# A state-space mixer's decay matmuls: two heads in one product, and the block between a sequence's two tiles for all heads at once

## The chip, the cores and the metric

The kernel runs on one core of a Trainium2 chip. It is one launch with everything in float32. The metric is device time in microseconds (us): the median of three runs.

## The reference, cut to what matters

The whole program is two transformer-like blocks, eight layers in a row. The change lies in the third layer, a state-space mixer. It has two passes ahead of it (a recurrent layer and a layer of eight experts) and five behind it. Of this layer the reference computes, for 4 sequences of 256 positions, 8 heads of width 64, and a state of width 64:

```
dt = softplus(dt + dt_bias);  A = -exp(A_log)
D_res = D[:, None] * h                     # skip path, per head
h = h * dt[..., None];  A_d = A * dt       # A_d: one decay exponent per position and head
L = exp(segment_sum(A_d))                  # L[l, s] = exp(sum of A_d over s < k <= l), 0 for s > l
y[l] = sum over s <= l of (C[l] . B[s]) * L[l, s] * h[s]   + D_res[l]
yn = norm_w * rmsnorm(y * silu(gate));  out = yn @ out_proj_w.T
```

The reference does the middle line in chunks of 32 positions and carries states between chunks; written out for a whole sequence it is the sum above. `B` and `C` are the same for all heads; the decay `L` differs by head.

## The kernel before, in words

The 1024 tokens are two groups (`g`), each of two sequences (`b`) of 256 positions; a sequence is two tiles of 128 positions on the 128 partitions. `NH` is 8, `NT` (tiles of a group) is 4. A pass of the mixer's last loop over one group and one sequence is called a **block** here; there are four: (g0,b0), (g0,b1), (g1,b0), (g1,b1).

Ahead of the blocks, each group has its convolution, its gate `sg` and its steps `dt` and exponents `ad` (`dtdt` and `dtad` in the profile). In the last loop a group first transposes `h` and forms `hdt` = h*dt (L365) and `hd` = D*h (L367).

A block then does this:

- `pG` (L373, L375): the products B.C for the three 128x128 pieces of the lower triangle: tile 0 to tile 0, tile 0 to tile 1, tile 1 to tile 1. `Gm` (L378) is that with the causal mask `m384` (called `m` in the profile), 384 columns wide.
- For each of the 8 heads, POOL scales the mask by the head's exponents into `au` (L394, 256 columns; L396, 128 columns). TensorE sums them along the positions into `pS`: L400 with the matrix `strict` (256 columns), L401 with `ones` (128 columns, adds the whole second tile's part to the middle piece), L402 with `strict` (128 columns). ScalarE takes the exponential (L404), VectorE multiplies by `Gm` (L405), and three matmuls of 64 columns (L383, L385, L387, the function `apply`) put the head's result into `pY[0]` and `pY[1]`. `apply` runs two heads behind the making of `L`.
- The tail: `yf` = pY + hd (L415, VectorE), times the gate (L417, POOL), the squares' sum (L419, ScalarE), `rs` (POOL, L101), transposes of `yf` (L430), their copies (L435), the output projection `pob` (L442, recorded under the helper's line L142), and the add to `x` (L443).

A float32 matmul is recorded as two TensorE instructions, so 32 matmuls of L400 appear as x64. `au` and `L` have four buffers each. PSUM tiles come from five banks in rotation (`mm_tile`), the two accumulators `pY` from three others.

The order of instructions on each engine isn't that of the text. A scheduler of the language lays them out when the kernel is built, by readiness under modelled durations. The trace shows it: POOL makes `au` for the next block's first heads ahead of this block's L417, and VectorE's normalisation of the next layer's input (`xn_f`, L117) for group 0 stands between two L405 of block (g1,b0). [...]

What comes after the mixer is a second pass of the eight-expert layer (L0f), whose instructions are laid out by the same scheduler, and then the second half of the program, whose order is written out by hand. The change touches neither.

Of the kernel before, what the change touches and what calls it, by code (L numbers as in the profile page):

```python
# [17 lines left out]
P = 128  # L18
# [4 lines left out]
S = 256  # L23
NT = TG // P
# [6 lines left out]
NH, HP, NS = 8, 64, 64  # L31
# [6 lines left out]
def two_blocks(ctx: ExitStack, tc: tile.TileContext, a: dict, out: bass.AP):  # L38
    nc = tc.nc

    const = ctx.enter_context(tc.tile_pool(name="const", bufs=1))
    small = ctx.enter_context(tc.tile_pool(name="small", bufs=3))
# [4 lines left out]
    def bank(tag, name):  # L47
        return ps.tile([P, 512], F32, tag=tag, name=name, bufs=banks_of[tag])
# [8 lines left out]
    def mm_tile(name, parts=P):  # L57
        return bank("mm" if mm_only[0] else next(mm_turn), name)[:parts]

    def acc_tile(name):  # L60
        return bank(next(acc_turn), name)
# [37 lines left out]
    def rsqrt(dst, src, n):  # L99

        nc.gpsimd.tensor_tensor(dst, src, neghalf[:, :n], ALU.pow)  # L101
# [37 lines left out]
    def project(dst, w, rhs, n=NC):  # L139

        for c in range(n):
            nc.tensor.matmul(dst, w(c), rhs(c), start=(c == 0), stop=(c == n - 1))  # L142
# [148 lines left out]
    def l0_attn_b(pool, win, wout, cw, nw, m384, strict, ones):  # L291
# [38 lines left out]
        for g in range(NG):  # L330
            v = keep[g][1]

            def new(n):
                return small.tile([P, NT, NH], F32, tag=f"dt{n}", name=f"dt{n}_{g}")
# [3 lines left out]
            z, w1, ln, eq, dt, ad = (new(n) for n in ("z", "w1", "ln", "eq", "dt", "ad"))  # L338
# [15 lines left out]
        for g in range(NG):  # L354
            hT, _, sg = keep[g]
            dt, ad = steps[g]
            hdt = pool.tile([P, NT, NH, HP], F32, tag="hdt", name=f"hdt_{g}")
            hd = pool.tile([P, NT, NH, HP], F32, tag="hd", name=f"hd_{g}")
            for t in range(NT):
                ph = mm_tile(f"ph_{g}_{t}")  # L360
                for j in range(4):
                    nc.tensor.transpose(
                        ph[:, j * P:(j + 1) * P], hT[j][:, t * P:(t + 1) * P], ident)
                ph = ph.rearrange("p (h q) -> p h q", h=NH)
                nc.vector.tensor_tensor(  # L365
                    hdt[:, t], ph, dt[:, t, :].unsqueeze(2).to_broadcast([P, NH, HP]), ALU.mult)
                nc.vector.tensor_tensor(  # L367
                    hd[:, t], ph, dres.unsqueeze(2).to_broadcast([P, NH, HP]), ALU.mult)
            for b in range(2):
                s0, s1 = b * S, b * S + P  # L370
                BT, CT = hT[4], hT[5]
                pG = mm_tile(f"pG_{g}_{b}")
                nc.tensor.matmul(pG[:, :S], BT[:, s0:s0 + P], CT[:, s0:s0 + S],  # L373
                                 start=True, stop=True)
                nc.tensor.matmul(pG[:, S:S + P], BT[:, s1:s1 + P], CT[:, s1:s1 + P],  # L375
                                 start=True, stop=True)
                Gm = pool.tile([P, S + P], F32, tag="Gm", name=f"Gm_{g}_{b}")
                nc.vector.tensor_tensor(Gm, pG[:, :S + P], m384, ALU.mult)  # L378
                pY = [acc_tile(f"pY{i}_{g}_{b}") for i in range(2)]

                def apply(h, L):
                    hs = slice(h * HP, (h + 1) * HP)
                    nc.tensor.matmul(pY[0][:, hs], L[:, :P], hdt[:, 2 * b, h, :],  # L383
                                     start=True, stop=True)
                    nc.tensor.matmul(pY[1][:, hs], L[:, P:S], hdt[:, 2 * b, h, :],  # L385
                                     start=True, stop=False)
                    nc.tensor.matmul(pY[1][:, hs], L[:, S:], hdt[:, 2 * b + 1, h, :],  # L387
                                     start=False, stop=True)

                behind = []  # L390
                for h in range(NH):
                    n = f"{g}_{b}_{h}"
                    au = pool.tile([P, S + P], F32, tag="au", name=f"au_{n}", bufs=4)
                    nc.gpsimd.tensor_scalar(  # L394
                        au[:, :S], m384[:, :S], ad[:, 2 * b, h:h + 1], None, ALU.mult)
                    nc.gpsimd.tensor_scalar(  # L396
                        au[:, S:], m384[:, S:], ad[:, 2 * b + 1, h:h + 1], None, ALU.mult)

                    pS = mm_tile(f"pS_{n}")
                    nc.tensor.matmul(pS[:, :S], strict, au[:, :S], start=True, stop=False)  # L400
                    nc.tensor.matmul(pS[:, P:S], ones, au[:, S:], start=False, stop=True)  # L401
                    nc.tensor.matmul(pS[:, S:S + P], strict, au[:, S:], start=True, stop=True)  # L402
                    L = pool.tile([P, S + P], F32, tag="L", name=f"L_{n}", bufs=4)
                    nc.scalar.activation(L, pS[:, :S + P], AF.Exp)  # L404
                    nc.vector.tensor_tensor(L, L, Gm, ALU.mult)  # L405
                    behind.append((h, L))
                    if len(behind) > 2:
                        apply(*behind.pop(0))
                for h, L in behind:
                    apply(h, L)  # L410
                ss = small.tile([P, 2], F32, tag="ss", name=f"ss_{g}_{b}")
                yf = pool.tile([P, 2, DI], F32, tag="yf", name=f"yf_{g}_{b}")
                for i in range(2):
                    t = 2 * b + i
                    nc.vector.tensor_tensor(  # L415
                        yf[:, i, :], pY[i], hd[:, t].rearrange("p h q -> p (h q)"), ALU.add)
                    nc.gpsimd.tensor_tensor(yf[:, i, :], yf[:, i, :], sg[:, t, :], ALU.mult)  # L417
# [499 lines left out]
    with ExitStack() as l0:  # L917
# [37 lines left out]
        with tc.tile_pool(name="b0", bufs=2) as pool:  # L955
            l0_attn_b(pool, win, wout, cw, nw, m384, strict, ones)
# [223 lines left out]
```

## Time and profile before

| what | value |
|---|---|
| median of 3 runs | 1007.36 us (1006.69 to 1009.06) |
| profiled execution, its own time | 1040.18 us |
| span of the profiled execution | 1038.5 us |
| mean granted TensorE clock over the span | 0.912 |
| TensorE busy | 854.4 us (82%) |
| VectorE, ScalarE, POOL busy | 529.0, 256.3, 280.9 us |
| mixer's four blocks, from the first `pS` to the last `pob` | about 194 to 296 us of the span |
| in the stretch 194 to 297 us: TensorE busy, POOL busy, mean clock | 89.84 us, 58.96 us, 0.83 |

How to read it: the profile is one execution, and its own time is 1.7 us more than its span, and 32.8 us more than the median of the runs without a profile. Busy time of TensorE is modelled at its ends, so the starts of successive instructions are the safer measure of what one costs. A line of a timeline gives the start in us, the duration in us, the engine, the source line, the operation, what it writes and reads, the shapes, the count, and in brackets how long the engine was idle before and what released it. "PEclk" in a window is the share of full speed that the clock of TensorE was granted.

### The profile page before, as it was taken

To read this page: it belongs to the slowest core of one execution; us is meant where nothing else is said; L and a number is where in the kernel's file an instruction comes from. 1 tells how busy PE (TensorE), PEld (TensorE's weight loads), DVE (VectorE), ACT (ScalarE), POOL (GpSimd) and SP (SyncE) were. 2 spreads that over 40 slices of the span, in tenths; PEclk is the share of its full clock that TensorE was granted. 3 is DMA by queue.
4 is the path that set the end of the run, shared out by engine and by line. 5 is a ranking of instruction groups with operands and counts; after the bars stand their busy time and mean duration, and the time that the engine had idled before them with its cause. 6 is when DMAs were issued, how large, how long until landed. Compare 5 with 4: busy or idle time off the path is not lost.

```text
span 1038.5 us, 10670 instructions
## 1 busy us (share of the span) xinstructions
PE 854.4 (82%) x3400; PEld 517.6 (50%) x3400; DVE 529.0 (51%) x1570; ACT 256.3 (25%) x470; POOL 280.9 (27%) x344
## 2 busy tenths in 40 slices
PE   4469999988989978988999776978988999866960
PEld 2235444777854433334337655854334336755850
DVE  5876666734346646326434433557525633523532
ACT  3410017522210021222225112212322224311210
POOL 3110000666410040120620325034120441144205
PEclk9779999988789979999999978989999999978995
DMA  8750000000000093000113526621000112435733
GB/s 296 247 183 0 1 0 1 1 1 1 1 1 1 0 265 101 1 21 1 66 46 112 157 98 192 183 86 56 1 0 1 47 66 71 128 126 167 208 109 98
DMA packets 61550, 81.47 MB, mean 78 GB/s; under 512 B 5928, under 2 KB 52528, under 8 KB 60976
## 3 DMA queue, kind: packets, MB, share of 16 engines
q1 hardware_dynamic: 43760, 52.48, 16.4%
q0 software_dynamic: 6144, 16.79, 5.1%
q10 hardware_dynamic: 11584, 11.46, 3.2%
q8 instruction: 29, 0.48, 0.2%
q14 instruction: 33, 0.27, 0.1%
HBM read 42.96 MB, written 37.75 MB: 78 GB/s over the span
## 4 chain that ended last, share of the span: by engine, by line
PE 61%; DVE 14%; issue 10%; POOL 6%; DMA 3%; ACT 3%; another core or an unknown queue 2%; POOLq 0%; ACTq 0%; SPq 0%; DVEq 0%
PE pe_f L142 11%; PE pgu_f L142 6%; PE pST_a L590 4%; PE py_f L841 3%; PE pS_a L555 3%; PE pST_b L590 3%; PE pS_b L555 2%; PE pob L142 2%; PE pcv L142 2%; PE pctx_a L606 2%; DVE ye_f L849 2%; DVE junk_b L561 2%; PE pctx_b L606 2%; PE po_a L142 2%
## 5 line engine op out<-in xcount | busy, mean ns | idle before, releaser
L142 PE MATMUL pgu_f<-gu,xT_f 128*128 128x192 f32 x512 | 107.2, 356 | 12.0 <-DVE ye_f L849 5.5
L142 PE MATMUL pe_f<-L0f_W_sb,xnT_f 128*128 128x512 f32 x256 | 115.7, 600 | 0.0
L142 PEld LDWEIGHTS pgu_f<-gu,xT_f 128*128 128x128 f32 x512 | 88.8, 203 | 23.6 <-DVE ye_f L849 18.1
L866 POOL DMA_INDIRECT yb_f<-done,bk_f x64 | 66.8, 1044 | 113.8 <-DMA xe_f<-sent 47.5
L284 DVE SCALAR_TENSOR_TENSOR x<-pe_f,comb_f,x 128x256 f32<-128x256 f32 x128 | 61.9, 484 | 39.6 <-PE pe_f L142 36.3
L783 POOL DMA_INDIRECT sent<-xn_f,to_f x64 | 63.0, 984 | 69.6 <-DVE full L770 51.5
L142 PEld LDWEIGHTS pe_f<-L0f_W_sb,xnT_f 128*128 128x128 f32 x256 | 46.6, 190 | 53.9 <-issue 51.6
L841 PE MATMUL py_f<-dw,hT_f 96*128 96x256 f32 x256 | 71.9, 408 | 1.5 <-ACT xT_f L818 1.2
L845 DVE TENSOR_TENSOR he_f<-he_f,pgu_f 128x192 f32<-128x192 f32 x64 | 22.5, 352 | 79.2 <-ACT he_f L835 65.0
L561 DVE CUSTOM_DVE_ANT_0 junk_a<-pS_a,tri 128x128 f32<-128x128 f32 (+1 forms) x128 | 45.8, 358 | 27.9 <-PE pS_a L555 22.2
L818 ACT COPY xT_f<-px_f 128x512 f32<-128x512 f32 x64 | 37.3, 586 | 89.2 <-PE px_f L815 67.3
L849 DVE COPY ye_f<-py_f 128x512 f32<-128x512 f32 x64 | 44.2, 691 | 26.7 <-PE py_f L841 9.6
L561 DVE CUSTOM_DVE_ANT_0 junk_b<-pS_b,tri 128x128 f32<-128x128 f32 (+1 forms) x128 | 45.8, 358 | 22.8 <-PE pS_b L555 17.1
L841 PEld LDWEIGHTS py_f<-dw,hT_f 96*128 96x128 f32 x256 | 50.0, 205 | 8.6 <-ACT xT_f L818 1.5
L590 PE MATMUL pST_a<-qm_a,kb_a 128*128 128x512 f32 x96 | 49.8, 625 | 5.3 <-DVE qm_a L577 4.6
L590 PE MATMUL pST_b<-qm_b,kb_b 128*128 128x512 f32 x96 | 49.3, 620 | 5.2 <-DVE qm_b L577 4.6
L595 POOL TENSOR_SCALAR_AFFINE_SELECT pT_a<-pT_a 128x512 f32<-128x512 f32 x32 | 20.4, 640 | 117.0 <-ACT pT_a L593 117.0
L593 ACT ACTIVATE pT_a<-pST_a 128x512 f32<-128x512 f32 x48 | 28.6, 597 | 92.4 <-PE pST_a L590 91.3
L593 ACT ACTIVATE pT_b<-pST_b 128x512 f32<-128x512 f32 x48 | 28.6, 597 | 90.6 <-PE pST_b L590 87.3
L815 PE MATMUL px_f<-ident,xe_f 128*128 128x128 f32 x256 | 41.3, 289 | 11.5 <-DMA xe_f<-sent 10.0
L555 PE MATMUL pS_b<-kb_b,qT_b 128*128 128x512 f32 x96 | 47.7, 601 | 2.8 <-DVE nmx L561 1.8
L555 PE MATMUL pS_a<-kb_a,qT_a 128*128 128x512 f32 x96 | 48.5, 609 | 1.0 <-DVE nmx L561 1.0
(297 smaller groups left out, 1436.4 us busy)
## 6 DMA issues: line engine op xcount, KB each, us to landing
xe_f<-sent SPq DMA_DIRECT2D x64, 256.0 KB
done<-ye_f SPq DMA_DIRECT2D x64, 256.0 KB
sent<-nil ACTq DMA_DIRECT2D x18, 512.0 KB
gu<-in_L1f_gate SPq DMA_DIRECT2D x4, 768.0 KB
gu<-in_L1f_up SPq DMA_DIRECT2D x4, 768.0 KB
dw<-in_L1f_down SPq DMA_DIRECT2D x4, 768.0 KB
L0f_W_sb<-in_L0f_W SPq DMA_DIRECT2D x4, 512.0 KB
L0b_in_sb<-in_L0b_in SPq DMA_DIRECT2D x1, 1160.0 KB
```

The costliest lines, as they stand in the source:

```text
L142: nc.tensor.matmul(dst, w(c), rhs(c), start=(c == 0), stop=(c == n - 1))
L284: nc.vector.scalar_tensor_tensor(x[g][:, t, :], pe[:, h * D:(h + 1) * D], comb[:, t, e:e + 1], x[g][:, t, :], ALU.mult, ALU.add)
L555: nc.tensor.matmul(pS.rearrange("p (s k) -> p s k", s=per), qT[:, c, q0:q0 + P], kb[:, s0:s0 + per, b * S:b * S + w], start=True, stop=True)
L561: nc.vector.tensor_tensor_reduce(out=junk[:, :w], in0=pS[:, i * w:(i + 1) * w], in1=tri[:, S - w:], scale=1.0, scalar=NEG, op0=ALU.add, op ...
L590: nc.tensor.matmul(pS, kb[:, s, k0:k0 + P], qm.rearrange("p c q -> p (c q)"), start=True, stop=True)
L593: nc.scalar.activation(pT.rearrange("p c q -> p (c q)"), pS, AF.Exp)
L606: nc.tensor.matmul(sums[0][32 * s:32 * s + 32, :], v[:, 2 * b + kt, s, :], told.pop(AG * kt + s).rearrange("p c q -> p (c q)"), start=(kt ...
L783: nc.gpsimd.indirect_dma_start(out=sent_to[g][t * TOPK + j], out_offset=bass.IndirectOffsetOnAxis(ap=to[:, t, j:j + 1], axis=0), in_=xn[:, ...
L815: nc.tensor.transpose(px[:, j * P:(j + 1) * P], xe[q][:, k, c * P:(c + 1) * P], ident)
L841: nc.tensor.matmul(py[:, k * D:(k + 1) * D], hT[q][:, k, :], dw[:, 2 * q + k, :], start=True, stop=True)
L849: nc.vector.tensor_copy(ye.rearrange("p k d -> p (k d)"), py)
L866: nc.gpsimd.indirect_dma_start(out=yb, out_offset=None, in_=done[g], in_offset=bass.IndirectOffsetOnAxis(ap=back[:, t, j:j + 1], axis=0), ...
```

## The change

Per group, two small matmuls and one exponential make `reach`: for each tile and head, the decay from a position to the end of its tile, and from the start of a tile to a position. The middle piece (tile 0 to tile 1) is then done for all heads in one matmul `pO` of 512 columns: its left factor is applied to `hdt` ahead of it (`left`, POOL), its right factor after it (`off`, VectorE), and the result is added to `hd`, the skip path. Per pair of heads, one POOL product makes `au` with 512 columns (two heads, two diagonal pieces), one matmul of 512 columns with `strict` makes `pS`, one exponential and one product follow, and `apply` has two matmuls per head instead of three, one pair behind. The matmul with `ones` is gone. `au` and `L` have three buffers of 512 columns instead of four of 384.

```diff
+            pe = mm_tile(f"pe_{g}").rearrange("p (k h) -> p k h", h=NH)
+            nc.tensor.matmul(pe[:, :NT], strict, ad, start=True, stop=True)
+            nc.tensor.matmul(pe[:, NT:2 * NT], m384[:, :P], ad, start=True, stop=True)
+            reach = small.tile([P, 2 * NT, NH], F32, tag="reach", name=f"reach_{g}")
+            nc.scalar.activation(reach, pe[:, :2 * NT], AF.Exp)
...
+                left = pool.tile([P, NH, HP], F32, tag="left", name=f"left_{g}_{b}")
+                nc.gpsimd.tensor_tensor(
+                    left, hdt[:, 2 * b],
+                    reach[:, 2 * b, :].unsqueeze(2).to_broadcast([P, NH, HP]), ALU.mult)
                 pY = [acc_tile(f"pY{i}_{g}_{b}") for i in range(2)]
...
+                def apply(h0, L):
+                    for h in (h0, h0 + 1):
+                        hs = slice(h * HP, (h + 1) * HP)
+                        for i in range(2):
+                            nc.tensor.matmul(pY[i][:, hs], L[:, h - h0, i, :],
+                                             hdt[:, 2 * b + i, h, :], start=True, stop=True)
+
+                behind = []
+                for h in range(0, NH, 2):
+                    n = f"{g}_{b}_{h}"
+                    au = pool.tile([P, 2, 2, P], F32, tag="au", name=f"au_{n}", bufs=3)
+                    nc.gpsimd.tensor_tensor(
+                        au, m384[:, :P].unsqueeze(1).unsqueeze(1).to_broadcast([P, 2, 2, P]),
+                        ad[:, 2 * b:2 * b + 2, h:h + 2].rearrange("p i h -> p h i")
+                        .unsqueeze(3).to_broadcast([P, 2, 2, P]), ALU.mult)
...
-                    au = pool.tile([P, S + P], F32, tag="au", name=f"au_{n}", bufs=4)
-                    nc.gpsimd.tensor_scalar(
-                        au[:, :S], m384[:, :S], ad[:, 2 * b, h:h + 1], None, ALU.mult)
-                    nc.gpsimd.tensor_scalar(
-                        au[:, S:], m384[:, S:], ad[:, 2 * b + 1, h:h + 1], None, ALU.mult)
...
-                    nc.tensor.matmul(pS[:, :S], strict, au[:, :S], start=True, stop=False)
-                    nc.tensor.matmul(pS[:, P:S], ones, au[:, S:], start=False, stop=True)
-                    nc.tensor.matmul(pS[:, S:S + P], strict, au[:, S:], start=True, stop=True)
-                    L = pool.tile([P, S + P], F32, tag="L", name=f"L_{n}", bufs=4)
-                    nc.scalar.activation(L, pS[:, :S + P], AF.Exp)
-                    nc.vector.tensor_tensor(L, L, Gm, ALU.mult)
+                    pS = mm_tile(f"pS_{n}")
+                    nc.tensor.matmul(pS, strict, au.rearrange("p h i l -> p (h i l)"),
+                                     start=True, stop=True)
+                    L = pool.tile([P, 2, 2, P], F32, tag="L", name=f"L_{n}", bufs=3)
+                    nc.scalar.activation(L.rearrange("p h i l -> p (h i l)"), pS, AF.Exp)
+                    nc.vector.tensor_tensor(
+                        L, L, Gm[:, 0:3:2, :].unsqueeze(1).to_broadcast([P, 2, 2, P]), ALU.mult)
                     behind.append((h, L))
-                    if len(behind) > 2:
+                    if h == 2:
+                        pO = mm_tile(f"pO_{g}_{b}")
+                        nc.tensor.matmul(pO, Gm[:, 1, :], left.rearrange("p h q -> p (h q)"),
+                                         start=True, stop=True)
+                        off = pool.tile([P, NH, HP], F32, tag="off", name=f"off_{g}_{b}", bufs=1)
+                        nc.vector.tensor_tensor(
+                            off, pO.rearrange("p (h q) -> p h q", h=NH),
+                            reach[:, NT + 2 * b + 1, :].unsqueeze(2).to_broadcast([P, NH, HP]),
+                            ALU.mult)
+                        nc.vector.tensor_tensor(hd[:, 2 * b + 1], hd[:, 2 * b + 1], off, ALU.add)
+                    if len(behind) > 1:
                         apply(*behind.pop(0))
```

More of the change, by code (lines that the diff above doesn't have):

```diff
@@ L376, in l0_attn_b @@
                                  start=True, stop=True)
-                Gm = pool.tile([P, S + P], F32, tag="Gm", name=f"Gm_{g}_{b}")
-                nc.vector.tensor_tensor(Gm, pG[:, :S + P], m384, ALU.mult)
-                pY = [acc_tile(f"pY{i}_{g}_{b}") for i in range(2)]
-                def apply(h, L):
-                    hs = slice(h * HP, (h + 1) * HP)
-                    nc.tensor.matmul(pY[0][:, hs], L[:, :P], hdt[:, 2 * b, h, :],
-                                     start=True, stop=True)
[L385 to L388, printed above, removed]
@@ L390, in l0_attn_b @@
-                behind = []
-                for h in range(NH):
-                    n = f"{g}_{b}_{h}"
-                    au = pool.tile([P, S + P], F32, tag="au", name=f"au_{n}", bufs=4)
-                    nc.gpsimd.tensor_scalar(
-                        au[:, :S], m384[:, :S], ad[:, 2 * b, h:h + 1], None, ALU.mult)
-                    nc.gpsimd.tensor_scalar(
-                        au[:, S:], m384[:, S:], ad[:, 2 * b + 1, h:h + 1], None, ALU.mult)
[L399 to L402, printed above, removed]
-                    L = pool.tile([P, S + P], F32, tag="L", name=f"L_{n}", bufs=4)
-                    nc.scalar.activation(L, pS[:, :S + P], AF.Exp)
-                    nc.vector.tensor_tensor(L, L, Gm, ALU.mult)
-                    behind.append((h, L))
-                    if len(behind) > 2:
+                Gm = pool.tile([P, 3, P], F32, tag="Gm", name=f"Gm_{g}_{b}")
@@ new lines, in l0_attn_b @@
+                nc.vector.tensor_tensor(
+                    Gm.rearrange("p i l -> p (i l)"), pG[:, :S + P], m384, ALU.mult)
+                left = pool.tile([P, NH, HP], F32, tag="left", name=f"left_{g}_{b}")
+                nc.gpsimd.tensor_tensor(
+                    left, hdt[:, 2 * b],
+                    reach[:, 2 * b, :].unsqueeze(2).to_broadcast([P, NH, HP]), ALU.mult)
+                pY = [acc_tile(f"pY{i}_{g}_{b}") for i in range(2)]
+                def apply(h0, L):
[4 more added lines that the diff above has]
+                                             hdt[:, 2 * b + i, h, :], start=True, stop=True)
@@ new lines, in l0_attn_b @@
+                behind = []
[8 more added lines that the diff above has]
+                    nc.tensor.matmul(pS, strict, au.rearrange("p h i l -> p (h i l)"),
+                                     start=True, stop=True)
+                    L = pool.tile([P, 2, 2, P], F32, tag="L", name=f"L_{n}", bufs=3)
+                    nc.scalar.activation(L.rearrange("p h i l -> p (h i l)"), pS, AF.Exp)
+                    nc.vector.tensor_tensor(
+                        L, L, Gm[:, 0:3:2, :].unsqueeze(1).to_broadcast([P, 2, 2, P]), ALU.mult)
+                    behind.append((h, L))
+                    if h == 2:
[3 more added lines that the diff above has]
+                        off = pool.tile([P, NH, HP], F32, tag="off", name=f"off_{g}_{b}", bufs=1)
+                        nc.vector.tensor_tensor(
+                            off, pO.rearrange("p (h q) -> p h q", h=NH),
[3 more added lines that the diff above has]
+                    if len(behind) > 1:
```

## The prediction

> **What bounds the kernel now.** I read the page first: TensorE is busy for 82% of the span and carries 61% of the chain that ended last. So the question is whether TensorE sets the pace where the change is made. I then asked for the timeline of block (g0,b1), where the pattern of one head repeats undisturbed:
>
> ```profile
> 228.20 0.92 POOL L394 TENSOR_SCALAR au<-m,dtad 128x256 f32<-128x256 f32 x1
> 228.21 0.49 ACT L404 ACTIVATE L<-pS 128x384 f32<-128x384 f32 x1 [1.06 <-PE pS L402]
> ...
> 228.63 0.65 PE L400 MATMUL pS<-au,strict 128*128 128x256 f32 x2
> 228.74 0.56 DVE L405 TENSOR_TENSOR L<-L,Gm 128x384 f32<-128x384 f32 x1 [0.99 <-ACT L L404]
> 229.10 0.67 POOL L396 TENSOR_SCALAR au<-m,dtad 128x128 f32<-128x128 f32 x1
> 229.12 0.38 PE L401 MATMUL pS<-au,ones 128*128 128x128 f32 x2
> 229.34 0.39 PE L402 MATMUL pS<-au,strict 128*128 128x128 f32 x2
> 229.56 0.33 PE L383 MATMUL pY<-hdt,L 128*128 128x64 f32 x2
> 229.73 0.39 PE L385 MATMUL pY<-hdt,L 128*128 128x64 f32 x2
> 229.75 0.92 POOL L394 TENSOR_SCALAR au<-m,dtad 128x256 f32<-128x256 f32 x1
> ...
> 229.96 0.39 PE L387 MATMUL pY<-hdt,L 128*128 128x64 f32 x2
> ```
>
> TensorE has no idle bracket. From start to start a product of 256 columns takes 0.49 us here, one of 128 columns 0.22, and one of 64 columns 0.17 to 0.22 (narrower is not cheaper). The next head's L400 starts at 230.18, so a head is 1.55 us of TensorE. POOL is nearly as full: its L394 starts at 228.20 and again at 229.75, also 1.55. ScalarE and VectorE wait for each head (1.06 and 0.99 us). Two engines are at their limit together, and the change relieves both.
>
> The blocks' tails are different. There TensorE waits for VectorE, then POOL (L415, then L417), and the clock falls:
>
> ```profile
> 206.00:208.00 2.00, 1.78 (x16) 1.00 0.00 0
> 208.00:210.00 2.00, 0.00 (x0) 0.91 0.00 0
> 210.00:212.00 2.00, 1.37 (x5) 0.50 0.00 0
> ...
> 216.00:218.00 2.00, 2.00 (x10) 0.89 0.03 8
> ```
>
> Columns: stretch, length, TensorE busy, granted clock, DMA share, GB/s. After 2 us without work the clock is 0.50 until about 217. The change leaves the tails as they are.
>
> Block (g1,b0) has a stall of its own: a normalisation of the next layer stands in VectorE's list ahead of an L405 and waits for POOL, which still has `au` ahead of it.
>
> ```profile
> 257.50 0.57 DVE L117 TENSOR_SCALAR xn_f<-x,mv_f,rstd_f 128x256 f32<-128x256 f32 x1 [5.46 <-POOL rstd_f L101]
> 258.00 0.55 DVE L405 TENSOR_TENSOR L<-L,Gm 128x384 f32<-128x384 f32 x1
> ...
> 258.60 0.48 PE L383 MATMUL pY<-hdt,L 128*128 128x64 f32 x1 [3.19 <-DVE L L405]
> ```
>
> That is 3.2 us idle, and the nine products after it run at half clock (0.43 us instead of 0.22: 1.9 us more).
>
> [...] The trace has L417, two inputs of 512 columns, at a median of 1.266 us, and that is my price for `au` and `left`. [...]
>
> ```profile
> 13.69 4.65 POOL L146 TENSOR_TENSOR x<-x,row 128x1024 f32<-128x1024 f32 x2
> 16.10 2.79 DVE L183 SCALAR_TENSOR_TENSOR mix<-xp,vec_sb,mixtmp 128x512 f32<-128x512 f32 x1 [2.63 <-ACT mixtmp L181]
> ```
>
> L183 has a median of 0.746 us; here it took 2.79, and ended 0.55 us after POOL did. With today's one-input L394 that is not seen: L405 above ran at 0.56 in the middle of one. So the change puts a new kind of collision into the loop. [...] the trace has 1.28 us each.
>
> **The change, part by part** (clock at full speed).
>
> 1. *`pS` for two heads in one.* Before, per pair: 2 x (0.49 + 0.22 + 0.22) = 1.86 us. After, 512 columns: 16 instructions of 512 columns in the expert layer took 7.06 us, 0.44 each, two for a product: 0.88. Gain 0.98 a pair.
> 2. *`apply`.* Before 2 x 0.62 = 1.24, after 4 x 0.22 = 0.88. Gain 0.36 a pair. A block so falls from 8 x 1.55 = 12.4 to 4 x 1.76 = 7.0.
> 3. *`pO`*, 512 columns, adds 0.88 a block. With it 7.9: a gain of 4.5 us a block, **18.0 us** for four.
> 4. *`pe`* adds two products of 32 columns a group, at the 0.22 of a narrow one: 0.9 us in all. They stand where TensorE is nearly full, so I charge them.
> 5. *`reach`*: 64 columns, one exponential a group, about 0.25 us on ScalarE, which is idle beside the blocks. But for g0 it comes while silu, exp and ln alternate (nine table loads between 155 and 197): it costs between nothing (beside another exp) and two table loads, 2.6 us, on an engine whose first L404 ends TensorE's wait at 197. I take 0.5.
> 6. *POOL.* A block had 8 x 1.55 = 12.4 us of `au`; it gets 4 x 1.27 plus `left` 1.27 = 6.3. POOL stops being a limit. L417 stood behind the next block's `au` for 0.7 us in two tails (ready at 208.06, started at 208.78): gain 1.4.
> 7. *Fewer covers.* A pair's latency from the end of `pS` is about 0.15 to drain, exp 0.60 (the attention's 128x512 L593 takes 0.597), L405 at 512 columns 0.69 (as L415), 0.09 of hand-over: 1.53. The cover is one `apply` and one `pS`, 1.76, so it fits, barely. For the last pair only one `apply` (0.88) covers it: 0.65 us idle a block, 2.6 in all. `off` and the add to `hd` (two of 0.69 on VectorE) fall where it is free; were they ahead of an L405 that TensorE awaits, 1.4 us a block.
> 8. *The collision.* [...] `au` is released as `pS` ends, which is when exp starts; 0.63 us later L405 comes and finds POOL with as much still to run. That is 0.2 us a pair in balance, or up to 0.6 where cover fails: between 0 and 10 us in all, and I take 2.5.
> 9. *The stall of (g1,b0)*, 3.2 + 1.9 us, has its cause in POOL's `au` queue. With half the queue I expect half of it to go: 2.5, between 0 and 5.1.
>
> Sum: -18.0 + 0.9 + 0.5 - 1.4 + 2.6 + 2.5 - 2.5 = **-15.4 us**. Nothing takes it back later: the expert layer after it is TensorE from 297 to 364 with the clock at 1.00, its weights lie in SBUF, and the weight loads of the second half start as it ends (365), so they move with it. The number of `mm_tile` calls changes by 2 - 4 x 3 = -10, twice the five banks, so the layer behind gets the same banks. Against the profiled time: 1040.2 - 15.4 = 1024.8. The runs without profile are 3.2% shorter, and I take the same gain less a trifle from them: 1007.4 - 15.4 = **992.0 us**.
>
> **The rivals.** *A, the forecast:* TensorE-bound blocks of 9.5 to 10.5 us in place of 13.5. *B, the collision bounds:* each L405 waits for a whole POOL product, as L183 did: 7.5 us more than item 8 takes, and two table loads, 2.1 more. Result 1002. For it: POOL and VectorE are released by the same event. Against it: `au` can be made ahead in the tail, with three buffers. *C, slower:* POOL's product is dear because both inputs are repeated reads (stride zero, in the innermost dimension for `ad`), which no row before has; L146 repeats in the outer dimension at 2.30 ns a column, no dearer than L417's 2.47. [...] At double price, 2.5 us, a block is 16.0: 4 x 3.6 = 14 us worse, less what items 6 and 9 give: 1018. *D, no effect:* the algebra does split (the decay across the tile border is the decay to the border times the decay from it), so the products are really gone; only a scheduler's order that leaves TensorE waiting for `pO` could eat them: 1007.
>
> **How the numbers follow.** A 0.68, B 0.20, C 0.08, D 0.04. Lowest for A: no collision, no final stall, the whole stall of (g1,b0) gone: 992.0 - 2.5 - 2.6 - 2.6 = 984.3; highest about 998. The range runs from 984 to 1002, which takes in A and most of B. A change of 0.2% (2 us) is about what a measurement here can tell. Faster by over 0.2%: A, nearly all of B, 0.87; within 0.2% 0.05; slower 0.08.
>
> **What would show it.** Right: `pS` as 32 instructions of 512 columns in all, starting 0.44 apart; a pair at 1.8 to 2.1 us; POOL's `au` near 1.27; L405's successor at 0.7 with some of 1.2 to 1.9; TensorE with some 210 fewer instructions; clock still 0.50 in four tails; first pass of the expert layer at about 281. Wrong: `au` above 1.8 us, or TensorE idle brackets of over 1 us in each pair, naming VectorE's product or `pO`.

## The result, and the profile after

The changed kernel takes **993.82 us** (median of 4 runs, 993.69 to 994.06) against 1007.03 us (4 runs, 1002.67 to 1009.06): ratio 0.9875, 95% interval 0.9842 to 0.9907. A second set gave 992.09 against 1004.8, ratio 0.9878 (0.9848 to 0.9908). The forecast was 992.0, with 984 to 1002 as its range.

Two lines of the page after: the span with the instruction count, and the busy times.

```profile
span 992.0 us, 10136 instructions
PE 827.2 (83%) x3192; PEld 483.7 (49%) x3192; DVE 533.1 (54%) x1562; ACT 250.6 (25%) x456; POOL 251.7 (25%) x300
```

TensorE has 208 instructions fewer, as announced ("some 210"). The two profiled spans differ by 46 us, which is not the gain. I therefore read a stretch that both profiles share: from the first transpose `ph` of the mixer's last loop to the first transpose `pt_f` of the layer after it. It is 104.59 us before and 90.09 us after: **14.5 us**. The first group's `pe` products stand just ahead of the first `ph` (0.36 us, from 196.13), so the stretch leaves them out; with them the gain is 14.1 us. By block, from one `pG` to the next (the last to `pt_f`):

| part | before | after | gain | forecast of the gain |
|---|---|---|---|---|
| first `ph` to first `pG` | 3.06 | 5.21 | -2.15 | about -1 (`pe`, `reach`) |
| (g0,b0) | 23.57 | 19.79 | 3.78 | 3.9 |
| (g0,b1) | 25.68 | 22.69 | 2.99 | 3.5 |
| (g1,b0), with its stall | 28.56 | 22.72 | 5.84 | 5.7 |
| (g1,b1) | 23.72 | 19.68 | 4.04 | 3.2 |

(The forecast column is items 1 to 3 and 6 to 9 of the prediction shared out by block; the second group's `pe` falls in block (g0,b1).)

Of the signs that the prediction gave, one failed: the first pass of the expert layer was to come at about 281 and came at 286.6. In this execution the mixer itself began later than in the first profile (the first `ph` at 196.5 instead of 191.6; see experiment 2).

This is the timeline of block (g0,b1) after, the block that was shown before. A line has start, duration, engine, source line, and in brackets the idle time before it and its releaser.

```profile
226.20 1.08 PE L411 MATMUL pS<-au,strict 128*128 128x512 f32 x2
...
227.12 1.00 PE L398 MATMUL pY<-hdt,L 128*128 128x64 f32 x8
...
227.32 0.60 ACT L414 ACTIVATE L<-pS 128x512 f32<-128x512 f32 x1 [2.36 <-PE pS L411]
227.43 1.47 POOL L405 TENSOR_TENSOR au<-m,dtad 128x512 f32<-128x512 f32 x1 [1.31 <-PE pS L411]
227.95 1.50 DVE L415 TENSOR_TENSOR L<-L,Gm 128x512 f32<-128x512 f32 x1
227.96 1.08 PE L411 MATMUL pS<-au,strict 128*128 128x512 f32 x2
...
229.50 1.10 PE L398 MATMUL pY<-hdt,L 128*128 128x64 f32 x8 [0.47 <-DVE L L415]
...
230.95 1.10 PE L398 MATMUL pY<-hdt,L 128*128 128x64 f32 x8 [0.35 <-DVE L L415]
```

A pair that nothing delays takes TensorE from 226.20 to 227.96, 1.76 us, exactly the sum of 0.88 and 0.88. The collision is there too: POOL's `au` runs from 227.43 to 228.90, VectorE's L415 comes at 227.95 and ends at 229.45, 0.55 us after POOL, as L183 did in the profile before. TensorE then waits 0.47 us, and 0.35 ahead of the last `apply`. The two groups in question, by line (minimum, median, maximum in ns):

```profile
L405 POOL TENSOR_TENSOR au<-m,dtad x16: 1040/1048/1592, 192.6 to 269.0; 128x512 f32<-128x512 f32 x16
L415 DVE TENSOR_TENSOR L<-L,Gm x16: 676/838/1531, 203.7 to 275.1; 128x512 f32<-128x512 f32 x16
```

Eight of the sixteen L415 run at their own length (0.68 to 0.69 us); the other eight, at 0.98 to 1.53, are held up; the four of block (g0,b1) ended 0.54 to 0.55 us after POOL's `au`. POOL is held up as well: L405 has a median of 1.048 us, and up to 1.592. The stall of block (g1,b0) has become shorter, and not gone. L117 stands ahead of L415 in VectorE's list and waits for POOL; the exponential that this L415 takes had ended at 254.06:

```profile
255.56 0.41 DVE L117 TENSOR_SCALAR xn_f<-x,mv_f,rstd_f 128x256 f32<-128x256 f32 x1 [2.32 <-POOL rstd_f L101]
255.88 0.69 DVE L415 TENSOR_TENSOR L<-L,Gm 128x512 f32<-128x512 f32 x1
...
256.62 1.42 PE L398 MATMUL pY<-hdt,L 128*128 128x64 f32 x8 [2.36 <-DVE L L415]
```

### The profile page after: what moved, and what is told of

It is laid out like the page before. It is cut to its first block, busy times and chain, and to the rows that moved or that the text cites. A ratio compares the mean times of both kernels' runs of the same rounds, so it can differ in the third digit from the quotient of the medians.

```text
span 992.0 us, 10136 instructions
## 1 busy us (share of the span) xinstructions
PE 827.2 (83%) x3192; PEld 483.7 (49%) x3192; DVE 533.1 (54%) x1562; ACT 250.6 (25%) x456; POOL 251.7 (25%) x300
## 4 chain that ended last, share of the span: by engine, by line
PE 60%; DVE 17%; issue 9%; POOL 5%; DMA 4%; ACT 3%; POOLq 0%; ACTq 0%; SPq 0%; DVEq 0%
PE pe_f L142 11%; PE pgu_f L142 7%; PE pST_a L611 4%; PE py_f L862 4%; PE pST_b L611 3%; PE pS_a L576 3%; PE pS_b L576 2%; PE pcv L142 2%; DVE ye_f L870 2%; PE pob L142 2%; PE pctx_b L627 2%; PE pctx_a L627 2%; PE po_a L142 2%; POOL sent L804 2%; DVE junk_b L582 1%
## 5 line engine op out<-in xcount | busy, mean ns | idle before, releaser
L142 PE MATMUL pgu_f<-gu,xT_f 128*128 128x192 f32 x512 | 102.8, 346 | 5.3 <-ACT xT_f L839 0.5
L142 PEld LDWEIGHTS pgu_f<-gu,xT_f 128*128 128x128 f32 x512 | 85.4, 197 | 16.9 <-DVE ye_f L870 15.0
L862 PE MATMUL py_f<-dw,hT_f 96*128 96x256 f32 x256 | 66.6, 384 | 0.3 <-DVE most_f L790 0.3
L878 DVE SCALAR_TENSOR_TENSOR x<-yb_f,wt_f,x 128x256 f32<-128x256 f32 x64 | 30.6, 479 | 36.0 <-DMA yb_f<-done,bk_f 35.8
```

The lines of the kernel that those rows point to most:

```text
L862: nc.tensor.matmul(py[:, k * D:(k + 1) * D], hT[q][:, k, :], dw[:, 2 * q + k, :], start=True, stop=True)
```

## The experiments

Times are medians; "gain" is against the changed kernel's 992.09 and its 90.13 us of stretch unless said otherwise. That kernel was timed together with experiments 7, 8 and the first half of 9. The others came in two later sets, in which the kernel before took 1005.11 (3, 4, 5, 10) and 1003.58 us (6, 11 and the second half of 9) instead of 1004.8, so differences of their medians from 992.09 are uncertain by about 1 us. The stretch is read in each run's profile. It is one execution each, but two profiles of one kernel agree in it within 0.2 us (104.59 and 104.75 before, 90.09 and 90.13 after), while unprofiled runs of one kernel differ by several us. So small effects are read from the stretch and checked against the medians.

One thing changes the stretch that an edit does not set directly: the clock. In every block the granted clock is 0.50 for a time, and in the blocks of these traces each such time was 3.41 us or two, three or four times that (6.83, 10.24, 13.65). So I count it in steps of 3.41 us; at a clock of 0.50 a step costs up to 1.7 us, half its length, where TensorE has work (an estimate). The steps in the four blocks with their tails:

| kernel | steps per block | in all |
|---|---|---|
| before (both profiles) | 2, 2, 4, 2 | 10 |
| after (both profiles) | 3, 2, 2, 2 | 9 |
| experiment 3 | 1, 2, 3, 1 | 7 |
| experiment 4 | 3, 2, 3, 2 | 10 |
| experiment 5 | 2, 2, 2, 2 | 8 |
| experiment 6 | 3, 2, 4, 2 | 11 |
| experiment 7 | 1, 2, 2, 2 | 7 |
| experiment 8 | 2, 2, 2, 2 | 8 |
| experiment 9, after and before | 3, 2, 2, 2 and 2, 2, 2, 2 | 9 and 8 |
| experiment 10 | 2, 2, 1, 2 | 7 |
| experiment 11 | 2, 1, 1, 1 | 5 |

A gain of 1 to 3 us in one stretch can therefore be a step of the clock as much as the wait that the edit removes. The main gain of 14 us is not of this kind: there it is one step of difference, 1.7 us at most. That the repeated profiles agree so well does not show how the stretch varies when the steps fall otherwise, since they had the same steps.

**1. The changed kernel again**, no edit.

> The changed kernel as it is, for a tight ratio and as the level for the others of this call. Theory (TensorE work removed from TensorE-bound blocks, part of it given back in collisions and waits): 0.985 to 0.990 of the kernel before, and the stretch from the first transposes of the mixer's last loop to the first transpose of the next layer about 90 us instead of 105. Rival (the difference of the two profiled spans, 46 us, is the gain): 0.955.

Ratio 0.9878, stretch 90.13 us. The theory's numbers came out.

**2. The kernel before, a second profile**, no edit.

> A second profile of the kernel before. The first one spans 1038.5 us where its unprofiled runs take 1002 to 1010. Theory that 32 us of that execution lie outside the mixer and have nothing to do with the change: the mixer's stretch (first transpose of the last loop to the first transpose of the next layer) again 104 to 105 us, the span nearer to 1005. Rival, that the change also shortens the second half of the program: span 1035 or more again.

The view of cores, span and clock:

```profile
core 0: 1000.2 us, clock 0.931
```

Its stretch is 104.75. So some 38 us of the first profile before were an affair of that one execution, outside the mixer. The difference of the first two spans (46 us) would have overstated the gain threefold. Set beside this profile, the first one loses most of them in two places of the second half, around `ph_f` and `pgu_f`: 16 us between 573 and 644 us of its span, and 17 us between 906 and 975. Why it was slow there stays open.

The spans mislead the other way as well: against this profile those of the changed kernel are only 8.3 and 9.1 us shorter. Its mixer began 4 us later in both its profiles (196.5 and 196.6 against 192.6), though TensorE's instructions up to there are the same; 1.7 us of that is one slow step of the clock near 175 us, which both profiles before lack.

**3. One of TensorE's products less, in the kernel before.**

```diff
-                    nc.tensor.matmul(pS[:, :S], strict, au[:, :S], start=True, stop=False)
-                    nc.tensor.matmul(pS[:, P:S], ones, au[:, S:], start=False, stop=True)
+                    nc.tensor.matmul(pS[:, :S], strict, au[:, :S], start=True, stop=True)
```

> The kernel before without its matmul with ones (L401), and nothing else; POOL's work is unchanged. It leaves out the second tile's part of the decay in the middle piece. Theory that TensorE sets the pace of a head: 32 products of 0.22 us go, 5 to 7 us faster than before, a head at 1.33 us. Rival, that POOL's au (0.92 + 0.60 = 1.52 us a head) is as much of a limit as TensorE's 1.55: a head stays at 1.52 and the gain is 1 us or less.

1000.71 us, ratio to before 0.9953 (0.9936 to 0.997); stretch 100.39, a gain of 4.2 us. The answer lies between the two. A head's period did fall, from 1.55 to 1.325 us (229.93 less 228.60 in its timeline). But the tail took it back. POOL's timeline at the end of block (g0,b1) (in this kernel L416 is the gate product, L429 the transposes):

```profile
232.52 0.92 POOL L394 TENSOR_SCALAR au<-m,dtad 128x256 f32<-128x256 f32 x1
233.42 0.59 POOL L396 TENSOR_SCALAR au<-m,dtad 128x128 f32<-128x128 f32 x1
234.00 0.91 POOL L394 TENSOR_SCALAR au<-m,dtad 128x256 f32<-128x256 f32 x1
234.90 0.59 POOL L396 TENSOR_SCALAR au<-m,dtad 128x128 f32<-128x128 f32 x1
235.47 2.48 POOL L416 TENSOR_TENSOR yf<-yf,sg 128x512 f32<-128x512 f32 x2
```

and TensorE's first transpose in the same tail:

```profile
236.77 0.47 PE L429 MATMUL pyt<-ident,yf 128*128 128x128 f32 x1 [3.92 <-POOL yf L416]
```

TensorE's last `apply` began at 232.47, but POOL still had `au` of the next block ahead of the gate product. From `pG` to the first transpose, the first two blocks are 15.36 and 15.80 us, before 15.42 and 15.84: no gain to speak of. The third gained 0.4 us, and the last, which has no next `au`, 1.7 (13.56 instead of 15.23). So up to the first transpose POOL was as much the bound of the first two blocks as TensorE. The other half of the 4.2 us came after the first transposes, where the clock had fewer slow steps.

**4. The split alone, one head at a time.** `pO`, `left`, `off` and `reach` as in the change; `au` by POOL's one-input products.

```diff
+                for h in range(NH):
+                    au = pool.tile([P, 2, P], F32, tag="au", name=f"au_{n}", bufs=4)
+                    for i in range(2):
+                        nc.gpsimd.tensor_scalar(
+                            au[:, i, :], m384[:, :P], ad[:, 2 * b + i, h:h + 1], None, ALU.mult)
...
+                    nc.tensor.matmul(pS[:, :S], strict, au.rearrange("p i l -> p (i l)"),
+                                     start=True, stop=True)
```

> The split alone, without the pairs: pO, left, off and reach as in the changed kernel, but one head per pS (256 columns), au by two one-input POOL products of 128 columns a head, three heads in flight. TensorE's columns are the same as in the changed kernel. Theory that relieving POOL is the other half of the change: POOL needs 2 x 0.60 = 1.2 us a head, a block is bound by 9.6 us of au (plus left 1.05), and about half of the gain is left: 0.990 to 0.995 of before. Rival, that TensorE's columns alone made the gain: as the changed kernel, 0.987 or less[...].

999.57 us, ratio 0.9927 (0.9893 to 0.9961); stretch 94.21. By the medians about six tenths of the gain, by the stretch seven (10.4 of 14.5 us), with TensorE's columns the same as in the changed kernel. POOL needs 4.07 us for seven of its products (0.58 each, 1.16 a head). A head's period in TensorE is 0.88 us as long as POOL's lead lasts, and 1.16 for the last heads of block (g0,b1) (226.77 to 227.93). The gate product again stands behind them: in block (g0,b1) TensorE waits 3.42 us for the first transpose, against 1.90 in the changed kernel. So the pairs seem to be worth the rest, through POOL. This is not isolated: the run also differs from the changed kernel in its cover (two heads), in its products with one input, beside which VectorE's (256 columns) took 0.42 to 0.57 us in this block, and by one step of the clock.

**5. Each matmul into `pS` twice**, in the changed kernel: the line is written twice.

> The changed kernel with each matmul into pS done twice (same result). Theory that TensorE still sets the pace of most of a block: 16 products of 0.88 us, 14 us, less the 4 to 6 us in which TensorE now waits inside the blocks: 8 to 12 us slower than the changed kernel. Rival, that POOL and VectorE, which shut each other out, now set the pace: 5 us or less.

1002.56 us, stretch 99.96: 9.9 us more in the stretch and 10.5 in the medians, of 14 us added, with one slow step fewer. TensorE still sets most of the pace; between a sixth and three tenths of an added product's length (2.4 to 4.1 of 14 us, by how much the step is worth) fall into waits that were there anyway.

**6. POOL's product for `au` twice**, in the changed kernel.

> The changed kernel with POOL's product for au done twice a pair (same result): 16 more products of 1.05 us, 16.8 us of POOL, each with two SBUF inputs. Theory that POOL has room in the changed blocks and costs only by shutting VectorE out and by the tail: 4 to 9 us slower than the changed kernel. Rival, that POOL still sets the pace as it did before: 14 us or more. Third, that POOL is hidden altogether: under 2 us.

999.25 us, 7.2 more; stretch 99.58, 9.5 more, of 16.8 us added. Neither hidden nor the full bound; up to 3.4 of the 9.5 us can be the two slow steps more. In block (g0,b0) the doubled list even reaches the length of before from `pG` to the first transpose (15.40 us).

**7. The exponential back into PSUM**, so that VectorE's product has one SBUF input.

```diff
-                    nc.scalar.activation(L.rearrange("p h i l -> p (h i l)"), pS, AF.Exp)
-                    nc.vector.tensor_tensor(
-                        L, L, Gm[:, 0:3:2, :].unsqueeze(1).to_broadcast([P, 2, 2, P]), ALU.mult)
+                    nc.scalar.activation(pS, pS, AF.Exp)
+                    nc.vector.tensor_tensor(
+                        L, pS.rearrange("p (h i l) -> p h i l", h=2, i=2),
+                        Gm[:, 0:3:2, :].unsqueeze(1).to_broadcast([P, 2, 2, P]), ALU.mult)
```

> The exponential is written back into its PSUM tile, so that VectorE's product L*Gm has one input in SBUF instead of two. Theory that POOL and VectorE shut each other out when both read two inputs from SBUF: every product of L takes 0.68 to 0.70 us (now 0.68 to 1.53, median 0.84), TensorE's waits for it fall, and the kernel gains 1.5 to 4 us on the changed one. Rival, that the waits come from the short cover of one pair and from the order of the lists: the products may get shorter, but the time stays within 1 us.

988.75 us, ratio 0.9846 (0.9817 to 0.9875), a gain of 3.3; stretch 87.11, a gain of 3.0. VectorE's line in this kernel:

```profile
L415 DVE TENSOR_TENSOR L<-pS,Gm x16: 673/691/692, 199.9 to 267.8; 128x512 f32<-128x512 f32 x16
```

and POOL's:

```profile
L405 POOL TENSOR_TENSOR au<-m,dtad x16: 1042/1047/1051, 188.7 to 262.1; 128x512 f32<-128x512 f32 x16
```

All sixteen of both now have nearly one length: VectorE's 0.692 us at most, with `L` from SBUF 1.531, and POOL's 1.051 at most, before 1.592. So in the changed kernel the two engines held each other up, and with this input in PSUM they did not. What that cost is less clear. TensorE's waits for L415 fell from 5.6 to 4.1 us, while two new ones ahead of `pS` came up (0.31 and 1.00 us, for other work of VectorE). 2.1 of the 3.0 us lie in block (g0,b0), where its wait of 1.16 us is gone and with it two slow steps.

**8. `apply` two pairs behind.**

```diff
-                    L = pool.tile([P, 2, 2, P], F32, tag="L", name=f"L_{n}", bufs=3)
+                    L = pool.tile([P, 2, 2, P], F32, tag="L", name=f"L_{n}", bufs=4)
...
-                    if len(behind) > 1:
+                    if len(behind) > 2:
```

> apply runs two pairs behind the making of L instead of one (L gets four buffers, the scratch of the squares one). Theory that the last pair of a block lacks cover: the waits of 0.35 to 0.57 us ahead of a block's last apply go, 1 to 2.5 us in all. Rival, that a product delayed by POOL sets the end of a block whatever the cover: less than 1 us.

988.8 us, ratio 0.9854 (0.9821 to 0.9886); stretch 87.16, a gain of 2.9. That is a little over the range given: 3.5 us of TensorE's waits for L415 are left of 5.6, since more cover also takes in products that POOL delays (L415 again up to 1.531 us), and block (g0,b0) had one slow step less.

**9. The next layer's normalisation behind the block's last sum**, in the changed kernel and in the kernel before. The same edit, an ordering on VectorE without a wait:

```diff
+        with tc.issue_after(hold[0]) if name == "f01_0" else ExitStack():
             for t in range(NT):
                 nc.vector.tensor_scalar(
                     xn[:, t, :], xg[:, t, :], mv[:, t, 0:1], rstd[:, t:t + 1],
```

> The next layer's normalisation of group 0 (L117) is queued on VectorE behind the last sum of block (g1,b0); nothing else changes in what is computed. Theory that the stall in this block still stands (2.36 us of TensorE waiting for VectorE, which waits for POOL) and costs its length and the slower clock after it: 2 to 4 us faster than the changed kernel. Rival, that the block's end is set by something else in reach of it: less than 1 us.

992.94 us, stretch 89.68: 0.45 us less in the stretch, nothing in the medians. The rival holds. The stall of 2.36 us is gone, but the freed product ran into POOL, and TensorE waited for that:

```profile
253.97 1.01 DVE L418 TENSOR_TENSOR L<-L,Gm 128x512 f32<-128x512 f32 x1 [0.86 <-ACT L L417]
...
255.03 1.10 PE L401 MATMUL pY<-hdt,L 128*128 128x64 f32 x8 [0.89 <-DVE L L418]
```

The first transpose came 1.56 us earlier after its `pG` (13.99 instead of 15.55), and the tail then took 0.76 us longer, since the clock came back later within it (`pob`'s sixteen instructions 5.27 us instead of 4.50); the last block is also 0.39 us longer.

> The kernel before with the next layer's normalisation of group 0 queued on VectorE behind the last sum of block (g1,b0). It prices the stall that stands in the profile of before (3.2 us idle and slow clock after it). Theory that it was worth 3 to 5 us: ratio 0.995 to 0.997. Rival, that POOL's list (au of the next block ahead of the gate product) ends the block at the same time anyway: less than 1.5 us.

1000.21 us, ratio to before 0.995 (0.9935 to 0.9965); stretch 101.79, a gain of 2.8 against the first profile (3.4 in the medians). Of the 5.1 us that the stall was reckoned at (3.2 + 1.9), only 1.6 came off between `pG` and the first transpose (20.06 to 18.50): TensorE was done with its last `apply` at 260.2, then waited 4.96 us for POOL's gate product. Most of the rest of the 2.8 lies in two tails (8.50 to 7.60, and 8.49 to 8.04); the clock was slow for two steps after this block instead of four. So a second wait stood behind the first and took most of what was freed.

**10. Edits 7, 8 and 9 together.**

> Exponential back into PSUM, apply two pairs behind, and the normalisation behind the block's last sum, all three on the changed kernel. Theory: the three waits are different ones, so the mixer's stretch goes from 90 us to 83 to 85 us and the kernel to 985 to 988. Rival, that they are the same wait seen three times (a late product of L): no better than the best of them, 988.8.

985.06 us, ratio 0.9798 (0.9757 to 0.9838); stretch 83.71. The sum of the three gains in the stretch is 3.0 + 2.9 + 0.45 = 6.4, and 6.4 came. That fits three different waits. The exact sum is in part chance, since the slow steps do not add up: two and one fewer for edits 7 and 8 alone, two fewer for all three.

**11. The gate product of the tail on VectorE as well.**

```diff
-                    nc.gpsimd.tensor_tensor(yf[:, i, :], yf[:, i, :], sg[:, t, :], ALU.mult)
+                    nc.vector.tensor_tensor(yf[:, i, :], yf[:, i, :], sg[:, t, :], ALU.mult)
```

> The changed kernel with the exponential back into PSUM, two pairs behind, the normalisation behind the last sum, and the gate product of the tail (L438) on VectorE instead of POOL. Theory that the tails are now the largest wait (TensorE idle about 1.9 and 0.5 us in each): the first transpose comes 0.58 us earlier in each block, the second about 0.5, so 1.5 to 3 us faster than with three edits, 982 to 984. Rival, that the clock stays at half speed for the same windows and swallows it: within 1 us of 985.

**978.97 us**, ratio to before 0.9745 (0.9717 to 0.9773); stretch 78.32, 5.4 us less than without this edit, more than I expected, and by another way: the first transposes were to come 0.58 us earlier in each block, and came 0.05 to 0.07 earlier. It beats both kernels. First the tail of block (g0,b1) with three edits, then with four:

```profile
225.26 2.49 POOL L444 TENSOR_TENSOR yf<-yf,sg 128x512 f32<-128x512 f32 x2 [2.10 <-DVE yf L440]
...
226.58 0.44 PE L457 MATMUL pyt<-ident,yf 128*128 128x128 f32 x2 [1.90 <-POOL yf L444]
...
227.80 1.54 PE L457 MATMUL pyt<-ident,yf 128*128 128x128 f32 x6 [0.79 <-POOL yf L444]
```

```profile
225.11 1.28 DVE L444 TENSOR_TENSOR yf<-yf,sg 128x512 f32<-128x512 f32 x2
...
225.94 1.57 PE L457 MATMUL pyt<-ident,yf 128*128 128x128 f32 x8 [1.85 <-DVE yf L444]
```

Two products take 1.28 us instead of 2.49. The first transpose still waits 1.85 us, instead of 1.90; the wait of 0.79 in the middle of the transposes is gone. From the first transpose to the next block the four parts are 7.39, 8.89, 6.60 and 6.41 us, before this edit 7.72, 10.81, 7.36 and 8.53: 5.1 of the 5.4 us lie there. One part of this is the wait in the middle of the transposes, 0.5 to 0.8 us in each tail. The other is the clock: the two tails with as many slow steps as before gained 0.3 and 0.8 us, the two with one step fewer 1.9 and 2.1. The same windows of block (g0,b1) with three edits, then with four (stretch, length, TensorE busy, granted clock, DMA share, GB/s):

```profile
227.00:230.40 3.40, 2.61 (x10) 0.53 0.00 0
230.40:234.00 3.60, 3.60 (x10) 0.50 0.02 5
```

```profile
227.00:230.40 3.40, 3.19 (x9) 0.50 0.02 5
230.40:234.00 3.60, 3.60 (x25) 1.00 0.00 0
```

Whether the shorter wait brings the clock back earlier, or the steps fell so by chance, one profile of each can't tell. With four edits one more slow step falls just behind the stretch (274.8 to 278.2).

## Why the prediction was right, step by step

- **The products (items 1 to 3): right.** A pair is 1.76 us. With the three waits removed (experiment 10), the blocks' ways from `pG` to the first transpose are 5.1, 5.0, 8.0 and 4.4 us shorter than before; the forecast was 4.5 each, before what items 6 and 9 add. But its condition was put too lightly. I wrote that both engines were at their limit and then booked the gain to TensorE, and 1.4 us to POOL. Experiment 3 shows that a relief of TensorE alone leaves the first transpose of a block where it was while POOL's list stands in front of the gate product, and experiment 4 that with POOL at 1.16 us a head the gate product still stands behind `au`. The change worked because it did both.
- **`pe` (item 4): right.** Two such products ran from 196.13 to 196.49, 0.36 us, against 0.44 reckoned; this pair lies outside the stretch.
- **`reach` (item 5): too small, and for another reason.** No table load was added (21 before and after): `reach` took the load that the first exponential of the blocks needed anyway. A load took 1.28 us, and the next activation started 0.02 us after it (L340 in the profile before, 189.62 to 190.90, then 190.92). What I had not seen is the PSUM bank. `pG` of the first block has a bank of the rotation to wait for, and it is that of `pe`, which is free when `reach` has read it:

```profile
201.42 0.22 ACT L362 ACTIVATE reach<-pe 128x64 f32<-128x64 f32 x1
...
201.70 0.70 PE L379 MATMUL pG<-cv,cv 64*128 64x256 f32 x2 [0.74 <-ACT reach L362]
```

  The way to the first `pG` is 2.15 us longer, where 0.5 was booked. Two products of 512 columns of `pS` now run ahead of `pG` (199.07 to 200.95), where one of 256 columns did before, so not all of it is loss.
- **POOL (item 6): its price was too high.** `au` has a median of 1.048 us, not 1.27. The delay of the gate product behind `au` is gone in the changed kernel, as forecast: ahead of its first gate product in each of the four blocks POOL waits for VectorE's sum.
- **Cover (item 7): right in kind and size.** Experiment 7, where every L415 took 0.67 to 0.69 us, shows the wait ahead of the last `apply` by itself: 0.61, 0.56 and 0.56 us in the three blocks without the stall, against 0.65. In the changed kernel it is mixed with item 8, so that the 2.9 us of experiment 8 next to 2.6 forecast are in part luck. The caution about `off` came true in block (g0,b0), as the next item shows.
- **Collision (item 8): right in kind; the size is partly luck.** Its 0.2 us a pair was an estimate of mine: 1.27 and 0.69 us one behind the other are 1.96, against TensorE's 1.76. 2.5 us taken, 3.0 to 3.3 regained by experiment 7, but not spread over the pairs: 2.1 us in the first block, 0.9 in the other three together. What the item did not foresee is small VectorE work: in the first block the last steps of group 1's `dtad`, and then `off`, stand between two L415, and POOL holds the former up.

```profile
203.74 4.15 POOL L405 TENSOR_TENSOR au<-m,dtad 128x512 f32<-128x512 f32 x3
...
205.90 1.03 DVE L350 TENSOR_TENSOR dtad<-dtdt,negA 128x32 f32<-128x32 f32 x1
...
206.86 0.68 DVE L423 TENSOR_TENSOR off<-pO,reach 128x512 f32<-128x512 f32 x1
207.46 0.98 DVE L415 TENSOR_TENSOR L<-L,Gm 128x512 f32<-128x512 f32 x1
...
208.50 3.17 PE L398 MATMUL pY<-hdt,L 128*128 128x64 f32 x16 [1.16 <-DVE L L415]
```

  L350 took 1.03 us here, and 0.175 for group 0. The L415 behind them had its exponential since 204.30. TensorE waits 1.16 us, and its clock falls a microsecond after it has resumed work (0.87 in 208 to 210 us, 0.50 after), and the last two pairs take 3.17 us, against 2.0 by the 1.00 us of eight in block (g0,b1). This is the block where experiment 7 gained most: 1.4 us from `pG` to the first transpose and 0.7 in the tail.
- **The stall (item 9): about right by size, with luck.** Half was to go; the wait fell from 3.2 to 2.36 us, and eight products ran at 1.42 us for 1.00, where nine had cost 1.9 us extra: 2.3 us, against 2.5. But the price of the stall was wrong. In the kernel before, the whole of it was worth 2.8 us and not 5.1 (experiment 9), because POOL's gate product stood behind it; so half of it could be gained only together with item 6. And the nine products were not all that the slow clock cost: it lasted four steps there instead of two. The hint that the rest was worth as much again was wrong: experiment 9 found 0.45.
- **The clock in the tails: right in kind.** It was 0.50 in four tails, as forecast, for two, two, four and two steps of 3.41 us before and three, two, two and two after. In block (g0,b0) after it fell at 209.5, 1.0 us after TensorE had resumed work from a wait of 1.16 us; that this wait is the cause was not shown. The prediction had no term for such steps; the change gave one more to block (g0,b0) and took two from (g1,b0).
- **Against the unprofiled runs:** 13.2 us in the medians and 14.5 in the stretch (14.1 with the first `pe`), 15.4 forecast; the interval of the ratio spans 9.4 to 15.9 us. The sum came out closer than its terms: the way to `pG` cost 1.2 us more than booked, the last block gave 0.8 us more. The rivals fell. B needed every L415 held up for a whole POOL product; half of them were, by 0.3 to 0.85 us. C needed `au` above 1.8 us, by my estimate that five of them and five of VectorE's 0.69, one behind the other, fill the old 12.4 us of a block; the median was 1.048. D asked TensorE to wait for `pO`: it waited 0.5 us once, ahead of it.

## What to carry to other kernels

When two engines are equally full, ask of each what stands behind its list: here relief of TensorE alone gained nothing up to the first transpose in the blocks whose tail sat behind POOL's work for the next block. Before an elementwise product of two SBUF tensors goes to POOL, look at what VectorE reads meanwhile; giving VectorE's product one input in PSUM took the collision away (0.692 us at most, before 1.531), and the exponential took no longer (medians of 0.582 and 0.597 us). And before you put a gain of 1 to 3 us down to a wait that is gone, compare the time at slow clock: with the tail's product on VectorE two of the four tails gained 0.3 and 0.8 us, and the two that had one slow step fewer 1.9 and 2.1.

## What the runs showed of the hardware that I had not expected

- POOL's products of two inputs with a repeated operand were cheaper: 1.048 us (`au`, both repeated) and 1.042 us (`left`, one repeated) against 1.266 us for two full inputs (L438), all 128x512. That the repetition is the cause was not tested; L438 also writes over one of its inputs.
- An exponential of 128x512 from PSUM back into PSUM took 0.582 us, into SBUF 0.597 (medians of L414, experiment 7 and the changed kernel).
- In the blocks, the slow times of TensorE's clock were 3.41, 6.83, 10.24 or 13.65 us (the table in the experiments). In block (g0,b0) of the changed kernel it fell 1.0 us after the end of a wait of 1.16 us.
- VectorE and POOL held each other up: VectorE's L415 took up to 1.531 us and POOL's `au` up to 1.592, and at most 0.692 and 1.051 with one of VectorE's inputs in PSUM.
- Beside the two-input `au` of the changed kernel, each L415 of block (g0,b1) ended 0.54 to 0.55 us after POOL's instruction. With the one-input `au` of experiment 3, the last five of VectorE's products in block (g0,b1) (L404 there) took 0.56 us where they began well inside a POOL instruction or ahead of one, and 0.77 to 0.78 where they began within 0.12 us of POOL's start (VectorE at 226.06 and POOL at 225.94, both at 228.71). Where VectorE was first by 0.04 us (227.38 and 227.42), POOL's instruction was the longer one, 1.31 for 0.92.
- The mixer began between 191.6 and 196.6 us in profiles whose instructions up to there are the same, while its own stretch repeated within 0.2 us: so a good part of the spread of the runs is made elsewhere.
